# Top-p attention in layer 0: shorter lists, one evaluation counted instead of run, one sum taken by a product, and the adjacency marks spread from the front on

## The chip, the cores and the metric

The kernel runs on one core of one Trainium2 chip. The metric is the device time of one execution in microseconds (us); each kernel is run three times and the median is taken. Engines are named as the profile names them: PE (TensorE matmuls; PEld are its weight loads), DVE (VectorE), ACT (ScalarE), POOL (GpSimd) and SP (SyncE, which issues most DMAs here).

## What is computed

Four graph layers on 4096 nodes of 256 features. Each takes x, normalises it, applies relu, runs a layer and adds the result to x. Only the first layer is touched by the change, and it has two steps (n = 0, 1):

```python
for n in range(STEPS):                       # STEPS = 2
    A = _top_p_attention(Xa, W1, W2, W3)     # 4096 x 4096, TOP_P = 0.9
    Xf = R @ Xf                              # R: adj plus the diagonal, rows scaled to sum 1; sparse
    Xa = A @ Xa
    Z = Z + Xf @ U1[n].T + Xa @ U2[n].T
```

Top-p attention takes the softmax of q k^T in each row, keeps the largest entries until their sum, without the entry itself, has reached 0.9, and divides by the sum of what was kept. About one entry in a thousand of adj is not zero. Layers 2 to 4 are a graph convolution, graph attention with four heads, and a second convolution.

## The kernel before, in words

**Sorting is avoided.** For each block b of 128 rows (32 blocks) the kernel has e = exp(logit − guess), 128x4096, and looks for the threshold t below which entries are dropped. It does so in these parts, named as in the lists of the order further down:

- *logits* (PE, L1148) and *exps* (ACT, L1162): e, in two halves.
- *evaluations* (`evaluate`, ACT, L1178): s*k* counts the entries over a trial threshold by the sum of signs, r*k* gives the mass below it by a relu, each with an accumulated sum. k = 0, 1 read 1024 columns (1.15 us each in the profile), k = 2, 3 read all 4096 (3.71 us).
- *updates* (`first`, `second`, `third`; DVE, L1200 to L1252): each turns s*k*, r*k* into a better trial threshold, in a series of instructions on 128x1. `first` belongs to k = 0, `second` to 1, `third` to 2. After k = 3, `bound` (L1255) turns the last evaluation into *hi*, a threshold that should be a little above the final one: `AHEAD` sets the margin.
- *below* (DVE, L1331): the entries under hi, with their sum; *segments* (L1339): the 8 largest in each of 16 segments of 256; *listing* (`order`, L1343 to L1353): from these 128, in rounds of 8 (a MAX8, and a MATCH_REPLACE8 with the load of its values), the `LIST` largest in falling order; *decide* (L1358 to L1381): where in that list the sum reaches the goal, so the exact threshold.
- *cut* (DVE, L1401) sets the dropped entries of e to zero; *drop* (L1403) removes ties where there are any.
- *flip* (PE transposes, L1469), *take* (ACT, PSUM to SBUF, L1475), *attend* (PE, L1484), in eight groups of four: the product A Xa. *attended* (ACT, L1493) scales it.

Then, for the block's rows, *turn_pe* (PE, L1512) transposes the new rows (xa) and the old (h), *turn* (ACT, L1517) copies them out, *keys_pe* and *keys* compute the next step's keys and queries, *xa_pe* and *h_pe* (`weighted`, PE, L1523) multiply by U1 and U2, *copy_xa* (ACT, L1542), *store_xa* (DVE add, L1546) and *store_h* (ACT, L1536) bring the results to SBUF and start their stores.

**Order of work.** The queues are in program order: `ORDERS` (L1096) lists by hand, for a *period*, what is issued. A name stands for a call with block b plus the offset behind `@` (`s0@3` is block b + 3). One period per block and three lead-in periods, −3 to −1, so DVE, ACT and PE work on four blocks at a time. The first list is step 0's, the second step 1's; step 1 also gathers the sparse product R Xf on POOL and applies it on PE. `some` and `along` (L921) interleave several generators instruction by instruction: `order` is listing beside bound, `maxima` segments beside bound, `third` an update beside decide, `first` an update beside the scale of the next product.

**PSUM and buffers that matter here.** The transposed tiles (pat, pt, tag pmisc) have two buffers, `take` three SBUF buffers, `pu` and the keys' bank share one tag (pr), hu has two.

**Marks.** Beside step 0 the kernel finds where adj is not zero: for each block, four quarters of adj (128x1024, 512 KB each) are loaded by SP, and `mark` (L1495) reduces each half of a quarter, 128x512, to the largest absolute value of each column group: eight instructions on DVE (L1498) per block, 256 in all. At the end of step 0 `listed_columns` (L748) turns the marks into lists.

**Check at the end.** `verify` (L1443) notes for every row that its list was long enough and its margin held; where a row's wasn't, `general_layers` computes all layers again in a plain way.

Of the kernel before, what the change touches and what calls it, by code (L numbers as in the profile page):

```python
# [92 lines left out]
SEG = 16  # L93
LIST = 48
AHEAD = 16.0
HUGE = 3e38


QUARTERS = 4
CHUNKS = 5  # L100
CAP = 32 * CHUNKS

# [552 lines left out]
def fast_layers(  # L655
# [81 lines left out]

    def load_adj(pool, ib):

        parts = []  # L740
        for c in range(0, NB, CA):
            t = pool.tile([P, CA, P], F32, name="adj", tag="adj")
            nc.sync.dma_start(t, adjt[ib, :, c : c + CA, :])
            parts.append(t)
        return parts

# [280 lines left out]

    def front(h0, kt, xs):

# [26 lines left out]
        for i in range(NB + LAG + 4):  # L1056
            o = i - LAG
            if i < NB:
                six = sm.tile([P, 6], F32, name="six")
                nc.vector.bn_stats(six, x0[i // 16][:, i % 16, :])  # L1060
                nc.vector.bn_aggr(spread_[:, i, :], six)
                if i % 4 == 3:
                    group = slice(i - 3, i + 1)
                    var = sm.tile([P, 4], F32, name="var4")
                    nc.vector.tensor_scalar_add(var, spread_[:, group, 1], LN_EPS)
                    nc.gpsimd.tensor_tensor(scale[:, group, 0], var, minus_half[:, :4], op=ALU.pow)
            if 0 <= o + 1 < NB:
                relu(o + 1)
# [29 lines left out]
    opened below attend2@-1 s1@2 some_maxima flip4@-1 r1@2 flip5@-1 attend3@-1 take4@-1 take5@-1 flip6@-1  # L1098
    second attend4@-1 take6@-1 attend5@-1 mark s2@2 mark maxima fill flip7@-1 attend6@-1 take7@-1 r2@2 attend7@-1
    order early logits0@3 attended@-1 mark turn_pe@-1 third fill turn@-1 exps0@3 keys_pe@-1 ties_pe logits1@3 cut  # L1100
    keys@-1 ties exps1@3 xa_pe@-1 s0@3 mark r0@3 drop copy_xa@-1 s3@2 store_xa@-1 flip0 mark flip1 mark
    take0 h_pe@-1 take1 fill first r3@2 flip2 attend0 mark mark attend1 store_h@-1 take2 flip3 take3 fill
    """,
# [3 lines left out]
    exps1@3 stood@-3 cut mix0 s0@3 laid@-3 s3@2 projected@-3 finish@-1 level@-2 mixed0 drop mix1 tabled@-3  # L1107
    r0@3 r3@2 attend7@-1 shifted@-2 fill first flip0 spread0 flip1 take0 heads@-1 other1 s1@3 attend0 take1 r1@3 flip2 flip3
    take2 attend1 take3 flip4 attend2 flip5 fill
# [16 lines left out]
    def layer0_step(n, va, kt, own, extra=None):  # L1126
# [43 lines left out]
        def evaluate(b, k, funcs=(AF.Sign, AF.Relu)):  # L1170

            s = state[b]
            width = PART if k < 2 else N
            if AF.Sign in funcs:
                s["signs"], s["gap"] = small("signs"), small("gap")
                s.setdefault("at", ones)
            for func in funcs:
                nc.scalar.activation(  # L1178
                    unread[:, :width],
                    s["e"][:, :width],  # L1180
                    func,
                    bias=s["at"],
                    scale=-1.0,
                    accum_out=s["signs"] if func == AF.Sign else s["gap"],
                )
# [15 lines left out]
        def measured(b, k):  # L1201
# [16 lines left out]
            return low, steep, goal  # L1218

        def stepped(to, m, t):  # L1220

# [33 lines left out]
        def bound(b):  # L1255

            s = state[b]
            low, steep, goal = yield from measured(b, 3)
            t = s["at"]
# [19 lines left out]
            yield  # L1279
            nc.vector.tensor_scalar_add(square[:, 1:2], square[:, 1:2], 1e-4)  # L1280
            yield
            nc.vector.scalar_tensor_tensor(
                square[:, 0:1], power, 1e-4, square[:, 0:1], op0=ALU.mult, op1=ALU.add
            )
# [23 lines left out]
            ahead, inverse = small("ahead"), small("inverse")  # L1308
            nc.vector.scalar_tensor_tensor(ahead, final, AHEAD, by, op0=ALU.mult, op1=ALU.mult)
            yield  # L1310
            nc.vector.reciprocal(inverse, goal)
            yield
            nc.vector.tensor_scalar(ahead, ahead, inverse, 3.0, op0=ALU.mult, op1=ALU.min)
            yield
# [28 lines left out]
        def listing(b):  # L1343

            first = state[b]["best"].rearrange("p k m -> p (k m)")
            rest = wk.tile([P, SEG * 8], F32, name="rest")
            listed = tops[:, b % 4, 1:]
            for k in range(0, LIST, 8):
                src = rest if k else first
                nc.vector.max(listed[:, k : k + 8], src)  # L1350
                yield
                if k + 8 < LIST:
                    nc.vector.match_replace(rest, listed[:, k : k + 8], src, 0.0)  # L1353
                    yield

            nc.gpsimd.tensor_copy(least[:, b : b + 1], listed[:, LIST - 1 :])

        def decide(b):  # L1358

            s, col = state[b], slice(b, b + 1)  # L1360
            listed, hi, room = tops[:, b % 4, 1:], end["hi"][:, col], end["room"][:, col]
            nc.vector.tensor_sub(room, s["low"], s["full_goal"])
            yield
            ahead_of = wk.tile([P, LIST], F32, name="ahead_of")
            nc.vector.tensor_tensor_scan(
                ahead_of, tops[:, b % 4, :LIST], tops[:, b % 4, :LIST], 0.0, op0=ALU.add, op1=ALU.bypass
            )
            yield
            out_ = wk.tile([P, LIST], F32, name="out_")
            nc.vector.tensor_scalar(out_, ahead_of, room, None, op0=ALU.is_ge)  # L1370
            yield
            kept = wk.tile([P, LIST], F32, name="kept")
            nc.vector.scalar_tensor_tensor(kept, out_, HUGE, listed, op0=ALU.mult, op1=ALU.add)
# [120 lines left out]

        def mark(b):  # L1495
            for q in range(QUARTERS):
                for part in (slice(0, CA // 2), slice(CA // 2, CA)):
                    nc.vector.tensor_reduce(  # L1498
                        marks[:, part, q, b],
                        state[b]["adj"][q][:, part, :],  # L1500
                        AX.X,
                        ALU.max,
                        apply_absolute_value=True,
                    )
                    yield

        def turn(b):
# [11 lines left out]
        def weighted(b, v):  # L1519

            pu = ps1.tile([P, 2, D], F32, name="pu", tag="pr")
            for k in range(DC):
# [4 lines left out]
                    start=(k == 0),  # L1527
                    stop=(k == DC - 1),
                )
            state[b]["pu"] = pu  # L1530

# [8 lines left out]
        def copy_xa(b):  # L1540
            t = state[b]["hu"] = own.tile([P, 2, D + 1], F32, name="hu", bufs=2)
            nc.scalar.copy(t[:, 0, :D], state[b]["pu"][:, 0, :])  # L1542

        def store_xa(b):
            rows, t = slice(b * P, (b + 1) * P), state[b]["hu"]
            nc.vector.tensor_add(t[:, 1, :D], va[:, b, :], state[b]["pu"][:, 1, :])  # L1546
            nc.sync.dma_start(heads_d[rows, :], t[:, 0, :D])
# [182 lines left out]
        def opened(b):  # L1730
            if n == 0 and 0 <= b < NB:
                state[b]["adj"] = load_adj(extra, b)
            if n == 1 and b in (0, NB // 2 + 1):
# [41 lines left out]
        def of_pair(f, r):  # L1775
# [5 lines left out]
            "drop": of_block(drop),  # L1781
            "mark": lambda b: some(line(mark, b), 1),
            "attended": of_block(attended),
# [6 lines left out]
            "copy_xa": of_block(copy_xa),  # L1790
            "store_xa": of_block(store_xa),
            "store_h": of_block(store_h),
# [26 lines left out]

        def period(b, fill=(), pieces=(0, 0, 0, 0)):  # L1820


            pieces = iter(pieces)
            for name, off in tables[max(b - NB + 1, 0)]:
                if name == "fill":
                    some(fill, next(pieces))
                else:
                    calls[name](b + int(off))

        def close(lists):  # L1830
# [29 lines left out]
            copy_xa(last)  # L1860
            store_xa(last)
            guesses = guess(1, pm)
# [8 lines left out]
    with ExitStack() as st:  # L1871
# [5 lines left out]
        for i, u in enumerate((u1t, u2t)):  # L1877
            wu.append(s0.tile([P, DC, 2, D], F32, name=f"wu{i}"))
            for n in range(2):
                nc.sync.dma_start(wu[i][:, :, 1 - n, :], u[n].rearrange("(c p) m -> p c m", p=P))  # L1880
        with tc.tile_pool(name="front", bufs=1) as xs, tc.manual_schedule(engines=MANUAL):
            guesses = front(h0, kt0, xs)
        own = st.enter_context(tc.tile_pool(name="own0", bufs=1))
        adj_pool = st.enter_context(tc.tile_pool(name="adj0", bufs=4))
        with tc.manual_schedule(engines=MANUAL):
            period, verify, close = layer0_step(0, h0, kt0, own, adj_pool)
            for b in range(-3, NB):
                period(b, guesses, {-3: (0, 0, 3, 0), -2: (3, 9, 9, 9)}.get(b, (0, 0, 0, 0)))
            lists = listed_columns(marks, e_pool.tile([P, N], F32, name="e"), ps)
            guesses = close(lists)  # L1890

    with ExitStack() as st:
# [3 lines left out]
        with tc.manual_schedule(engines=MANUAL):  # L1896
# [3 lines left out]
            for b in range(-3, NB + 2):  # L1900
                period(b, fill, pieces.get(b, (0, 0, 0, 0)))
                if b == -1:
# [412 lines left out]
```

## Time and profile before

| | us |
|---|---|
| three runs, median (lowest to highest) | 3152.24 (3150.27 to 3155.07) |
| the profiled execution | 3154.33 |
| its span, first to last instruction | 3152.2 |
| PE busy | 2524.1 (80%) |
| DVE busy | 2555.9 (81%) |
| ACT busy | 2242.7 (71%) |
| POOL busy | 1274.5 (40%) |
| mean granted TensorE clock | 0.934 |

By the trace's cuts (L1401) the span has these stages: a front that normalises and makes keys (0 to 106), the lead-in of step 0 (106 to 193), step 0's periods (193 to 1188), its close and the lead-in of step 1 (1188 to 1326), step 1's periods (1326 to about 2400), and the other three layers (from 2400 on).

How to read it: the views used are the page, *windows* (busy time of each engine in a stretch, then the granted clock, the DMA's share and GB/s), *waits* (engine and line, what it waited for, us in total, times, longest), and the *timeline* of one engine (start, duration, instruction, count, and in brackets the idle time before it with what ended it). A shape is written partitions x elements. In the timeline, neighbouring instructions of one line are joined, and a duration runs over the next instruction's start where the engine overlaps them, so "spacing" (start to start) is said where it is meant.

### The profile page before, as it was taken

To read this page: it belongs to the slowest core of one execution; us is meant where nothing else is said; L and a number is where in the kernel's file an instruction comes from. 1 tells how busy PE (TensorE), PEld (TensorE's weight loads), DVE (VectorE), ACT (ScalarE), POOL (GpSimd) and SP (SyncE) were. 2 spreads that over 40 slices of the span, in tenths; PEclk is the share of its full clock that TensorE was granted. 3 is DMA by queue.
4 is the path that set the end of the run, shared out by engine and by line. 5 is a ranking of instruction groups with operands and counts; after the bars stand their busy time and mean duration, and the time that the engine had idled before them with its cause. 6 is when DMAs were issued, how large, how long until landed. Compare 5 with 4: busy or idle time off the path is not lost. (4 is left out here: it accounts for less than half of the span.)

```text
span 3152.2 us, 44347 instructions
## 1 busy us (share of the span) xinstructions
PE 2524.1 (80%) x12468; PEld 1893.4 (60%) x12468; DVE 2555.9 (81%) x9611; ACT 2242.7 (71%) x3436; POOL 1274.5 (40%) x1350
## 2 busy tenths in 40 slices
PE   6658888888888887398998988999876776888666
PEld 5336556565656665176767667677765554788444
DVE  3389999999999998899999999999982776899200
ACT  3589999999999953888888888998932123899100
POOL 1000000000000000278888846566654775775576
PEclk9779999999999999699999999999988998999888
DMA  3012232322223233034444433334333874554575
GB/s 125 9 48 88 78 98 77 96 81 84 88 76 98 78 111 98 29 111 126 126 125 126 124 106 107 104 97 127 109 94 95 266 212 136 150 157 123 177 210 163
DMA packets 213852, 357.05 MB, mean 113 GB/s; under 512 B 33879, under 2 KB 147036, under 8 KB 213596
## 3 DMA queue, kind: packets, MB, share of 16 engines
q1 hardware_dynamic: 169100, 237.74, 23.6%
q0 software_dynamic: 43520, 116.14, 13.6%
q8 instruction: 102, 1.67, 0.2%
q14 instruction: 154, 1.26, 0.1%
q10 hardware_dynamic: 976, 0.23, 0.0%
HBM read 290.85 MB, written 63.13 MB: 112 GB/s over the span
## 5 line engine op out<-in xcount | busy, mean ns | idle before, releaser
L1178 ACT ACTIVATE unread<-e,next_pair 128x4096 uint8<-128x4096 f32 (+1 forms) x384 | 1098.2, 2860 | 50.0 <-DVE next_pair L1229 45.3
L1484 PE MATMUL pa<-va,at 128*128 128x256 f32 x2048 | 498.7, 392 | 60.3 <-DVE t L1615 45.0
L1484 PE MATMUL pa<-h,at 128*128 128x256 f32 x2048 | 472.2, 381 | 17.5 <-ACT at L1475 17.5
L1484 PEld LDWEIGHTS pa<-va,at 128*128 128x128 f32 x2048 | 384.8, 195 | 142.4 <-ACT at L1475 61.0
L1341 POOL COPY eighth<-best 128x16 f32<-128x16 f32 x64 | 21.6, 337 | 1039.2 <-DVE best L1339 824.9
L1475 ACT COPY at<-pat 128x512 f32<-128x512 f32 x512 | 285.1, 583 | 197.8 <-PE pat L1469 192.7
L1484 PEld LDWEIGHTS pa<-h,at 128*128 128x128 f32 x2048 | 377.3, 190 | 69.3 <-ACT at L1475 24.4
L1339 DVE MAX8 best<-near 128x8 f32<-128x256 f32 x1024 | 404.5, 418 | 3.2
L1469 PE MATMUL pat<-ident,e 128*128 128x128 f32 x2048 | 291.7, 279 | 100.4 <-ACT at L1475 55.1
L1469 PEld LDWEIGHTS pat<-ident,e 128*128 128x128 f32 x2048 | 247.3, 144 | 185.9 <-ACT at L1475 79.3
L835 POOL DMA_INDIRECT vg<-v_d,column x320 | 306.1, 956 | 118.7 <-issue 90.6
L1148 PE MATMUL pl<-kt,qb 64*128 64x512 f32 x1024 | 279.2, 656 | 75.8 <-ACT e L1162 75.7
L1162 ACT ACTIVATE e<-pl,minus_guess 128x1024 f32<-128x1024 f32 x256 | 282.9, 1111 | 44.7 <-PE pl L1148 34.3
L850 PE MATMUL acc<-vg,ac 128*128 128x256 f32 x768 | 228.9, 445 | 93.1 <-DMA vg<-v_d,column 73.0
L1331 DVE SCALAR_TENSOR_TENSOR near<-e,end_hi 128x4096 f32<-128x4096 f32 x64 | 286.7, 4480 | 0.1
L1401 DVE SCALAR_TENSOR_TENSOR e<-e,end_t 128x4096 f32<-128x4096 f32 x64 | 286.6, 4478 | 0.0
L835 POOL DMA_INDIRECT vg<-far_d,column x160 | 250.4, 1565 | 60.2 <-issue 41.8
L835 POOL DMA_INDIRECT vg<-mixed_d,column x160 | 219.1, 1369 | 86.2 <-issue 44.6
L850 PEld LDWEIGHTS acc<-vg,ac 128*128 128x128 f32 x768 | 157.9, 220 | 158.6 <-DMA vg<-v_d,column 100.6
L850 PE MATMUL pr<-vg,ac 128*128 128x257 f32 (+1 forms) x768 | 197.5, 409 | 56.1 <-issue 33.8
L2141 PE MATMUL acc<-u,tabg 128*65 128x128 f32 x1536 | 194.5, 281 | 45.3 <-DVE u L2126 44.2
L850 PEld LDWEIGHTS pr<-vg,ac 128*128 128x128 f32 x768 | 150.4, 202 | 104.8 <-issue 39.5
(554 smaller groups left out, 4483.7 us busy)
## 6 DMA issues: line engine op xcount, KB each, us to landing
adj<-in_adjt SPq DMA_DIRECT2D x128, 512.0 KB
ac<-adjc_d SPq DMA_DIRECT2D x96, 384.0 KB
adjc_d<-ac SPq DMA_DIRECT2D x32, 384.0 KB
vg<-v_d SPq DMA_DIRECT2D x64, 128.0 KB
targets<-steep_d SPq DMA_DIRECT2D x32, 256.0 KB
vg<-v_d,column POOLq DMA_INDIRECT x320, 4.0
table_d<-tab SPq DMA_DIRECT2D x32, 132.0 KB
tabg<-table_d SPq DMA_DIRECT2D x32, 132.0 KB
```

Of the source, the lines that this page charges most:

```text
L835: nc.gpsimd.indirect_dma_start(out, None, rows, bass.IndirectOffsetOnAxis(ap=index, axis=0))
L850: nc.tensor.matmul(acc, ac[:, k, :], v[:, k, :], start=(k == 0), stop=(k == CHUNKS and not own))
L1148: nc.tensor.matmul(pl[:, r, :], s["qb"][rows], kt[rows, j * 512 : (j + 1) * 512], start=True, stop=True,)
L1162: nc.scalar.activation(s["e"][:, j * 1024 : (j + 1) * 1024], pl.rearrange("p r c -> p (r c)"), AF.Exp, bias=minus_guess[:, b : b + 1], acc ...
L1178: nc.scalar.activation(unread[:, :width], s["e"][:, :width], func, bias=s["at"], scale=-1.0, accum_out=s["signs"] if func == AF.Sign else ...
L1331: nc.vector.scalar_tensor_tensor(near, s["e"], end["hi"][:, b : b + 1], s["e"], op0=ALU.is_lt, op1=ALU.mult, accum_out=s["low"])
L1339: nc.vector.max(best[:, k, :], near[:, k * (N // SEG) : (k + 1) * (N // SEG)])
L1401: nc.vector.scalar_tensor_tensor(s["e"], s["e"], last, s["e"], op0=ALU.is_ge, op1=ALU.mult, accum_out=s["held"])
L1469: nc.tensor.transpose(pt[:, k, :], s["e"][:, c * P : (c + 1) * P], ident)
L1475: nc.scalar.copy(at, s["pt", g])
L1484: nc.tensor.matmul(s["pa"], s["at", g][:, k, :], va[:, c, :D], start=(c == 0), stop=(c == NB - 1))
L2141: nc.tensor.matmul(s["acc"][:, h, :], s["tab"][:, k, h * (DK + 1) : (h + 1) * (DK + 1)], s["u"][:, k, h, :], start=(k == 0), stop=(k == CH ...
```

## The change

It changes layer 0 in these places.

- **Marks.** A generator, `marking`, walks over all 128 quarters in order; it keeps the loads up to four quarters ahead and makes one reduce of a whole quarter (128x8 from 128x1024) per step. `mark` in the list takes one step of it. 16 steps are taken in the front, 4 more in the front's end, 36 by the `fill` places of the lead-in periods, and three in each period from block 0 on (before: eight half reduces in each), until the 128 are used up.
- **r3 is not run.** The relu evaluation for k = 3 leaves the lists, in both steps. `counted` takes its place: it works the mass out from the last two counts (s2 and s3), the two thresholds and the mass before.
- **Lists of 32 and 40.** `LIST` = 48 becomes 32 in step 0 and 40 in step 1: four and five rounds of listing instead of six. The margin of `bound` has another formula, with `AHEAD` 11 in place of 16 and a term from the last step's size.
- **store_xa's add becomes a product.** In `weighted(b, 0)` one more matmul adds the identity times the block's old rows into the second half of pu, and `copy_xa` copies both halves (128x512 in place of 128x256). The add on DVE goes.
- **copy_xa is issued earlier**, directly after exps1 and xa_pe and ahead of s0, r0 and drop; before, it stood behind them. The two stores come with it.

The diff, cut to its core:

```diff
-LIST = 48
-AHEAD = 16.0
+LISTS = (32, 40)
+LIST = max(LISTS)
+AHEAD = 11.0
+SPREAD = 0.5
...
-    def load_adj(pool, ib):
+    def marking(pool, marks):
         parts = []
-        for c in range(0, NB, CA):
-            t = pool.tile([P, CA, P], F32, name="adj", tag="adj")
-            nc.sync.dma_start(t, adjt[ib, :, c : c + CA, :])
-            parts.append(t)
-        return parts
+        for k in range(NB * QUARTERS):
+            while len(parts) < min(k + ADJ_BUFS, NB * QUARTERS):
+                b, q = divmod(len(parts), QUARTERS)
+                parts.append(pool.tile([P, CA, P], F32, name="adj"))
+                nc.sync.dma_start(parts[-1], adjt[b, :, q * CA : (q + 1) * CA, :])
+            b, q = divmod(k, QUARTERS)
+            nc.vector.tensor_reduce(
+                marks[:, :, q, b], parts[k], AX.X, ALU.max, apply_absolute_value=True
+            )
+            yield
...
+            if i >= 10 and i % 2 == 0:
+                some(marked, 1)
...
-    second attend4@-1 take6@-1 attend5@-1 mark s2@2 mark maxima fill flip7@-1 attend6@-1 take7@-1 r2@2 attend7@-1
-    order early logits0@3 attended@-1 mark turn_pe@-1 third fill turn@-1 exps0@3 keys_pe@-1 ties_pe logits1@3 cut
-    keys@-1 ties exps1@3 xa_pe@-1 s0@3 mark r0@3 drop copy_xa@-1 s3@2 store_xa@-1 flip0 mark flip1 mark
-    take0 h_pe@-1 take1 fill first r3@2 flip2 attend0 mark mark attend1 store_h@-1 take2 flip3 take3 fill
+    second attend4@-1 take6@-1 attend5@-1 mark s2@2 maxima fill flip7@-1 attend6@-1 take7@-1 r2@2 attend7@-1
+    order early logits0@3 attended@-1 turn_pe@-1 third fill turn@-1 exps0@3 keys_pe@-1 ties_pe logits1@3 cut
+    keys@-1 ties exps1@3 xa_pe@-1 copy_xa@-1 s0@3 r0@3 mark drop s3@2 flip0 flip1
+    take0 h_pe@-1 take1 fill first flip2 attend0 mark attend1 store_h@-1 take2 flip3 take3 fill
...
-    r0@3 r3@2 attend7@-1 shifted@-2 fill first flip0 spread0 flip1 take0 heads@-1 other1 s1@3 attend0 take1 r1@3 flip2 flip3
+    r0@3 attend7@-1 shifted@-2 fill first flip0 spread0 flip1 take0 heads@-1 other1 s1@3 attend0 take1 r1@3 flip2 flip3
...
+        def counted(b):
+            s = state[b]
+            pair, before, goal = s["next"], s["before"], s["full_goal"]
+            s["pair"] = pair
+            t, low, twice, steep = pair[:, 0:1], pair[:, 1:2], small("twice"), small("steep")
+            mass, gap = small("mass"), small("gap")
+            nc.vector.tensor_add(mass, t, before[:, 0:1])
+            yield
+            nc.vector.scalar_tensor_tensor(
+                mass, s["signs"], s["signs2"], mass, op0=ALU.subtract, op1=ALU.mult
+            )
+            yield
+            nc.vector.tensor_scalar(twice, s["signs"], float(N), t, op0=ALU.add, op1=ALU.mult)
+            yield
+            nc.vector.scalar_tensor_tensor(
+                low, mass, 0.25, before[:, 1:2], op0=ALU.mult, op1=ALU.add
+            )
+            yield
+            nc.vector.scalar_tensor_tensor(low, goal, 0.1, low, op0=ALU.mult, op1=ALU.max)
+            yield
+            nc.vector.scalar_tensor_tensor(gap, twice, 0.5, low, op0=ALU.mult, op1=ALU.subtract)
+            yield
+            nc.vector.scalar_tensor_tensor(
+                steep, gap, -0.33 / 0.465, twice, op0=ALU.mult, op1=ALU.add
+            )
+            yield
+            s["gap"] = gap
+            return low, steep, goal
...
         def bound(b):
-            low, steep, goal = yield from measured(b, 3)
+            low, steep, goal = yield from counted(b)
...
-            nc.vector.scalar_tensor_tensor(ahead, final, AHEAD, by, op0=ALU.mult, op1=ALU.mult)
+            nc.vector.scalar_tensor_tensor(m, m, -1.0, m, op0=ALU.mult, op1=ALU.max)
+            yield
+            nc.vector.scalar_tensor_tensor(
+                ahead, final, AHEAD / (4.0 * SPREAD), by, op0=ALU.mult, op1=ALU.mult
+            )
...
-            nc.vector.tensor_scalar(ahead, ahead, inverse, 3.0, op0=ALU.mult, op1=ALU.min)
+            nc.vector.scalar_tensor_tensor(ahead, ahead, inverse, m, op0=ALU.mult, op1=ALU.add)
+            yield
+            nc.vector.tensor_scalar(ahead, ahead, 4.0 * SPREAD, 3.0, op0=ALU.mult, op1=ALU.min)
...
-            for k in range(0, LIST, 8):
+            for k in range(0, LISTS[n], 8):
...
-                if k + 8 < LIST:
+                if k + 8 < LISTS[n]:
...
         def weighted(b, v):
...
-                    stop=(k == DC - 1),
+                    stop=(k == DC - 1 and v > 0),
                 )
+            if v == 0:
+                nc.tensor.matmul(pu[:, 1, :], ident, va[:, b, :], start=False, stop=True)
...
         def copy_xa(b):
             t = state[b]["hu"] = own.tile([P, 2, D + 1], F32, name="hu", bufs=2)
-            nc.scalar.copy(t[:, 0, :D], state[b]["pu"][:, 0, :])
-
-        def store_xa(b):
-            rows, t = slice(b * P, (b + 1) * P), state[b]["hu"]
-            nc.vector.tensor_add(t[:, 1, :D], va[:, b, :], state[b]["pu"][:, 1, :])
+            nc.scalar.copy(t[:, :, :D], state[b]["pu"])
+            rows = slice(b * P, (b + 1) * P)
             nc.sync.dma_start(heads_d[rows, :], t[:, 0, :D])
             nc.sync.dma_start(base_d[rows, :], t[:, 1, :D])
...
+            early = {
+                -3: ((0, 2), (0, 2), (3, 2), (0, 2)),
+                -2: ((3, 4), (9, 4), (9, 4), (9, 4)),
+                -1: ((0, 3), (0, 3), (0, 3), (0, 3)),
+            }
             for b in range(-3, NB):
-                period(b, guesses, {-3: (0, 0, 3, 0), -2: (3, 9, 9, 9)}.get(b, (0, 0, 0, 0)))
+                period(b, (guesses, marked), early.get(b, ((0, 0),) * 4))
```

## The prediction

> **What bounds the kernel now.** The profiled execution took 3154.3 us (span 3152.2), 2.1 above the median of the runs shown, 3152.24; the sum is made on 3154.3. The page's chain follows only the last 16 us of the span, so I read by stage: the windows view for which engine is full, the waits of each stage, then the timeline of one period, engine by engine. The windows (PE, PEld, DVE, ACT, POOL busy, then the granted clock) of step 0 and step 1:
>
> ```profile
> 600.00:800.00 200.00, 171.76 (x836) 121.36 (x835) 188.89 (x768) 184.56 (x242) 2.73 (x18) 1.00 0.26 84
> 1330.00:1700.00 370.00, 326.21 (x1569) 253.44 (x1570) 358.25 (x1350) 326.13 (x370) 296.53 (x249) 0.96 0.42 121
> ```
>
> In step 0 DVE is 94% busy, but it isn't the bound: the waits of 300 to 1100 us show it stopped once in each period by ACT, and ACT hardly ever by DVE.
>
> ```profile
> DVE hu L1546 <- ACT hu L1542: 26.2, 24, 1.2
> ACT unread L1178 <- DVE m L1301: 0.3, 1, 0.3
> ```
>
> A period is the distance of two cuts (L1401): 32.41 us on average over the 28 from 226.97 to 1134.40. ACT's timeline in one of them (start, us, ...):
>
> ```profile
> 646.31 0.59 ACT L1517 COPY zt<-pt 128x512 f32<-128x512 f32 x1 [0.74 <-PE pt L1512]
> ...
> 651.80 1.13 ACT L1178 ACTIVATE unread<-e,ones 128x1024 uint8<-128x1024 f32 x1
> ...
> 654.20 0.35 ACT L1542 COPY hu<-pu 128x256 f32<-128x256 f32 x1
> 654.46 3.71 ACT L1178 ACTIVATE unread<-e,next_pair 128x4096 uint8<-128x4096 f32 x1
> ...
> 658.16 1.06 ACT L1475 COPY at<-pat 128x512 f32<-128x512 f32 x2
> 659.10 3.72 ACT L1178 ACTIVATE unread<-e,next_pair 128x4096 uint8<-128x4096 f32 x1
> ...
> 663.27 1.10 ACT L1475 COPY at<-pat 128x512 f32<-128x512 f32 x2
> ```
>
> In the order of the list these are turn, s0 and r0, copy_xa, s3, take0 and take1, r3, take2 and take3. PE beside it:
>
> ```profile
> 650.21 1.98 PE L1523 MATMUL pu<-wu,zt 128*128 128x512 f32 x4
> 653.46 1.09 PE L1469 MATMUL pat<-ident,e 128*128 128x128 f32 x8 [1.27 <-DVEq L1408]
> 655.06 1.98 PE L1523 MATMUL pu<-wu,zt 128*128 128x512 f32 x4 [0.51 <-DVE hu L1546]
> 658.78 0.66 PE L1469 MATMUL pat<-ident,e 128*128 128x128 f32 x4 [1.74 <-ACT at L1475]
> ...
> 663.93 1.99 PE L1484 MATMUL pa<-h,at 128*128 128x256 f32 x8 [0.60 <-ACT at L1475]
> ...
> 678.16 0.44 PE L1512 MATMUL pt<-ident,xa 128*128 128x128 f32 x2
> ```
>
> They are xa_pe, flip0 and flip1, h_pe, flip2, attend2, turn_pe. From flip2 to turn_pe PE works without a gap except for attend2, which waits for take2 behind r3. flip2 needs one of two PSUM buffers, so it waits for take0; take0 stands behind s3. The loop closes: turn_pe to zt's start 0.69, to s0 5.49 (both exps, keys), s0 and r0 2.40, copy_xa 0.26, s3 3.70, take0 to flip2 0.62: 13.16 (645.62 to 658.78). PE from flip2 to the next turn_pe: 19.4, of which 0.76 is the wait for take2 (weights' wait included) and 18.65 PE's own. 13.16 + 18.65 + 0.76 = 32.57, the measured period within 0.2. So **step 0 is bound by a loop through ACT and PE**; DVE has 1.2 us of slack.
>
> Step 1 is different: windows of its periods show DVE 97% busy, its waits with DVE ahead hold 0.3 to 0.8 us, and POOL's gathers run beneath. There DVE is the bound.
>
> **Part by part.**
>
> *r3 goes* (L1178, 3.71 + 0.19, 64 times), and counted adds six small DVE instructions. In step 0 the loop contains only 0.76 of r3, the wait of attend2: −0.76. The six (0.12 spacing each, rows of 0.15 us) are taken in turn with the rounds of listing, whose gaps hold most of them; I take 0.1 to 0.4 a period, with no end in step 0, where DVE has the slack.
>
> *copy_xa moves ahead of s0 and r0, and becomes 128x512.* Before, it stood behind r0, when xa_pe (650.21 to 652.19) had long ended, and waited for nothing. Now ACT reaches it at the end of exps1 (651.80, turn_pe + 6.18) and must wait for xa_pe: + 6.57, + 0.44 for the added product (two records as L1512's, 0.22 apart), + 0.13 to a copy's start as in the rows: turn_pe + 7.05. Wait: **+0.87**. Queued behind it on ACT: s0, r0, s3, take0, and so flip2. The wide copy costs 0.48 in place of 0.26 (L1517's copy of that size, by its spacing): +0.22. Bounds: +0.9 to +1.2 for both. The stores of heads_d and base_d move ahead with it. On SP they can stand behind a load of a quarter that waits for the reduce just before it; hu has two buffers, so a store has most of a period before a copy misses it: 0.
>
> *Loop without a change of clock:* 32.57 − 0.76 + 0.87 + 0.22 = 32.9, or +0.33 a period, +10 us over 28 periods: nothing of r3's 3.9 us is won, as what follows is s3 before take0.
>
> *The clock.* After the change PE runs flip0, flip1 and h_pe earlier: flip0 and flip1 no longer wait for the cut, as DVE is ahead, and h_pe waits for copy_xa, not for L1546. It ends at turn_pe + 10.3 (copy_xa's end 7.5, flips' 1.0, 1.83), flip2 starts at turn_pe + 13.16 + 1.09 = 14.25: PE stands still for **3.95 us** in each period, where it stood for 1.74 before. What that does shows in step 1. Windows and PE there:
>
> ```profile
> 1617.00:1620.40 3.40, 3.40 (x16) 2.15 (x15) 3.30 (x15) 2.93 (x5) 2.79 (x3) 1.00 0.96 309
> 1620.40:1623.80 3.40, 1.12 (x6) 0.63 (x4) 3.37 (x6) 3.37 (x3) 3.40 (x1) 1.00 0.20 63
> 1623.80:1627.20 3.40, 3.29 (x8) 2.67 (x9) 3.40 (x3) 3.33 (x5) 2.63 (x6) 0.52 0.49 135
> ...
> 1623.91 4.53 PE L850 MATMUL pr<-vg,ac 128*128 128x257 f32 x12 [2.40 <-issue]
> ```
>
> A window with PE busy for a third (one gap of 2.40) is followed by one of the granted clock at half, and the same twelve products took 4.53 in it, 2.88 just before: 1.65 lost. Over the trace the granted clock changes on a grid of 3.41 us; full-speed windows busy for 42% or less are nearly all followed by a half-speed one, those from 49% on in step 0 never (its clock is 1.00 all through). A gap of 3.95 leaves some window 58% idle or more wherever the grid falls, so the drop should come in nearly every period, right where flip2 starts the PE part of the loop. A half-speed window holds 1.7 us less work; laid out against the grid the period becomes 34.7, **+2.2 × 28 = +62** in place of +10. Bounds: +10 (no drop) to +80 (a second window in one period of three).
>
> The Trainium skill ("TensorE: Matmul & The Clock Gate", "HAM oscillation — how this bites in real kernels") rules that only PE idle gaps above some 3.4 us bring the throttle back, a wholly idle window by its Part 1. By that rule a gap of 3.95 covers a whole window in (3.95 − 3.41) / 3.41 = 16% of phases, an estimate of +9 on top of the +10; this trace throttled after 2.3 to 2.4, so the trace decides.
>
> *Marks.* 256 reduces of 0.60 spacing become 128 of 128x1024: nearest row L797 (same elements read, 1.22 us), about 1.15 by spacing. The work is equal; it moves. Sixteen go into the front, where DVE is 30 to 45% busy: 0, and its tail 0.8. Of the early ones 28 fall in periods −2 and −1 (135 to 193), DVE busy 34.4 of 58 there: 34.4 + 28 × 1.15 − 2 (marks already there) = 64.6, 6.6 over; and DVE can't fill the gaps at its six updates, where it waits about 1 to 1.3 us each for s and r (rows of 0.94 and 1.06): +7. **+14**, bounds +5 (r3's 3.9 gone from ACT lets the chain catch up) to +20 (512 KB loads supplied late, 1.8 us each). Afterwards three a period, under the slack: 0.
>
> *Lists of 32 and 40:* two rounds less in step 0, one in step 1 (MAX8, load, replace: 0.72 spacing). Step 0: 0, DVE isn't the bound. Step 1: −0.72 − 0.04 + 0.2 for counted = −0.55 × 30 = **−16.5** (bounds −8 to −24: PE's half clocks there may take some back). r3's going gives ACT 3.9 us that step 1 doesn't wait for: 0.
>
> *Product for the add L1546* (423 ns): its stall of 1.23 on DVE goes; late next is the third update's wait for r2. Loop: counted above. *Close:* −0.4; *step 1's start:* −2 (r3 before s1, a longer chain in bound). *Layers 1 to 3:* 0.
>
> **Sum:** 3154.3 + 0.8 + 14 + 62 − 16.5 − 0.4 − 2 = **3212 us**.
>
> **Rivals.**
>
> *The clock holds.* Step 0's lowest windows now (49% busy) passed, and if the gap comes out at 2 us, not 3.95, so do these. Then 3154.3 + 0.8 + 14 + 10 − 16.5 − 2.4 = 3160, with the bounds of marks and step 1 3144 to 3172. It decides when PE's gap before flip2 stays under about 2.
>
> *Faster: DVE is step 0's bound after all.* 94% busy speaks for it. If take0 is not what flip2 waits for, the period falls with DVE's: 32.41 − 1.44 (two rounds) − 1.6 (the add and its stall) − 1.3 (marks, 8 × 0.60 to 3 × 1.15) + 0.4 = 28.5, or −110: 3150 (the sum without step 0's loop) − 110 = 3040; with half of it kept, as PE and ACT have 27 and 26 us of work each, 3095. Against it: flip2 and attend2 wait for ACT in these periods, and DVE's stall is itself a wait for ACT. It decides when flip2 starts less than about 12 us behind turn_pe.
>
> *A step is repeated.* Were a list too short for one row, the general path would compute the layers again, by estimate at least the 3154 us of the listed way. Worked out from the inputs, no row needs more than 28 of 32 and 38 of 40 entries; 1%.
>
> **How the numbers follow.** Forecast (half clock in most periods) 65%, own range 3190 to 3232; clock holds 17%; faster 13%; other slower ones 4%, repeat 1%. The range 3140 to 3236 leaves out the faster case, the repeat and a few per cent of tails. What a measurement here can tell from no change is 0.2%, 6.3 us: 3146 to 3158.5 around the median. The clock case lies half in it: same 8%; faster 13% + 2%; slower the rest.
>
> **What would show it.** In step 0: cuts about 34.7 apart; PE idle 3.9 before flip2, for ACT at L1475; granted clock near 0.95 in windows now at 1.00; ACT waiting 0.8 at copy_xa for PE; DVE idle some us a period, for ACT. Step 1's periods 0.5 shorter. The first cut (now 193.44) near 207 to 210. It is wrong if the clock of step 0 stays 1.00, or if its period falls under 32.

## The result, and the profile after

The changed kernel takes 3204.99 us (median of four runs, 3202.86 to 3207.61) against 3151.55 for the kernel before on the same chip: ratio 1.0168, 95% interval 1.0151 to 1.0186. It is slower by 53 us; the forecast was 3212. The profiled execution has a span of 3200.8 us, 48.6 more than before's. Between the same cuts of both traces:

| stage | before, us | after, us | difference | forecast |
|---|---|---|---|---|
| front and lead-in, up to the first cut | 193.4 | 211.2 | +17.8 | +14.8 |
| step 0, first cut to 30th | 941.0 | 1005.2 | +64.2 | +62 |
| end of step 0, close, lead-in of step 1 | 192.0 | 188.8 | −3.2 | −2.4 |
| step 1, first cut to last | 1035.0 | 1013.4 | −21.6 | −16.5 |
| the rest (layers 2 to 4) | 790.8 | 782.2 | −8.6 | 0 |

(In the changed kernel the cut is L1449, evaluations L1190, flip L1517, attend L1532, take L1523, turn L1553, xa_pe and h_pe L1559 with the added product L1567, copy_xa L1580, marks L750, below L1379.)

The windows of steps 0 and 1 after (PE, PEld, DVE, ACT and POOL busy, granted clock, DMA share, GB/s):

```profile
600.00:800.00 200.00, 168.57 (x783) 123.00 (x784) 164.81 (x689) 154.79 (x209) 2.73 (x18) 0.94 0.21 65
1390.00:1760.00 370.00, 318.45 (x1529) 244.25 (x1530) 360.88 (x1457) 289.00 (x349) 299.62 (x253) 0.95 0.43 121
```

In step 0 no engine is full any more: DVE went from 94% to 82%, ACT from 92% to 77%, and the period still grew from 32.41 to 34.74. Work left, and the loop got longer. The clock is 0.94 where it was 1.00. In step 1 DVE is as full as before (97.5%). The waits of step 0, from 300 to 1150 us (engine, what it waited for, us in total, times, longest):

```profile
PE pat L1517 <- ACT at L1523: 108.7, 24, 4.7
DVE twice L1220 <- ACT unread L1190: 83.7, 49, 4.1
DVE pair L1222 <- ACT unread L1190: 48.6, 49, 1.0
ACT hu L1580 <- PE pu L1567: 21.5, 24, 1.0
```

PE waits 4.5 us for take0 once in each period, where it waited 1.7; DVE now waits for ACT's evaluations; copy_xa waits 0.9 for xa_pe. ACT's and PE's timelines over one period show the gap and what comes behind it:

```profile
666.01 0.59 ACT L1580 COPY hu<-pu 128x512 f32<-128x512 f32 x1 [0.76 <-PE pu L1567]
...
669.04 3.71 ACT L1190 ACTIVATE unread<-e,next_pair 128x4096 uint8<-128x4096 f32 x1
...
672.75 1.05 ACT L1523 COPY at<-pat 128x512 f32<-128x512 f32 x2
```

```profile
666.98 1.88 PE L1559 MATMUL pu<-wu,zt 128*128 128x512 f32 x4
673.37 1.12 PE L1517 MATMUL pat<-ident,e 128*128 128x128 f32 x4 [4.51 <-ACT at L1523]
674.28 4.53 PE L1532 MATMUL pa<-h,at 128*128 128x256 f32 x16
...
707.61 1.12 PE L1517 MATMUL pat<-ident,e 128*128 128x128 f32 x4 [4.51 <-ACT at L1523]
708.51 6.17 PE L1532 MATMUL pa<-h,at 128*128 128x256 f32 x16
```

h_pe ends at 668.86, flip2 starts at 673.37. The sixteen products behind it take 4.53 us in this period and 6.17 in the next; at full clock they took 3.62. Half speed runs from 672.7 to 676.1 here. Two stretches across the gap, which lie 1.1 us behind the grid on which the clock changes, so that each holds a part of it:

```profile
670.40:673.80 3.40, 0.43 (x2) 0.43 (x3) 3.37 (x4) 3.40 (x5) 0.00 (x0) 0.84 0.29 67
673.80:677.20 3.40, 3.40 (x14) 2.91 (x13) 3.30 (x6) 1.08 (x3) 0.00 (x0) 0.66 0.49 175
```

The granted clock is at half for one stretch of 3.4 us in most periods: these cuts are 34.24 to 34.6 apart. In about every sixth period it stays at half for 6.8, and the cuts are 35.9 apart (35.0 in the last such case). In these six the gap reaches further into the first half-speed stretch: PE is busy for 77 to 78% of it in five of them and for 26% in the sixth, while after stretches busy for 80% or more the clock came back. Half-speed time in the 28 periods is 116 us; before it was 2.

### The profile page after: what moved, and what is told of

It is laid out like the page before. It is cut to its first block, busy times and chain, and to the rows that moved or that the text cites. A ratio compares the mean times of both kernels' runs of the same rounds, so it can differ in the third digit from the quotient of the medians.

```text
span 3200.8 us, 44193 instructions
## 1 busy us (share of the span) xinstructions
PE 2553.5 (80%) x12532; PEld 1929.9 (60%) x12532; DVE 2511.2 (78%) x9547; ACT 2022.3 (63%) x3308; POOL 1266.8 (40%) x1350
## 5 line engine op out<-in xcount | busy, mean ns | idle before, releaser
L1190 ACT ACTIVATE unread<-e,next_pair 128x4096 uint8<-128x4096 f32 (+1 forms) x320 | 859.7, 2686 | 103.5 <-DVE next_pair L1271 71.2
L1532 PE MATMUL pa<-va,at 128*128 128x256 f32 x2048 | 495.5, 389 | 55.7 <-DVE t L1650 47.8
L1523 ACT COPY at<-pat 128x512 f32<-128x512 f32 x512 | 287.8, 581 | 391.8 <-PE pat L1517 386.3
L1532 PE MATMUL pa<-h,at 128*128 128x256 f32 x2048 | 511.9, 405 | 0.0
L1532 PEld LDWEIGHTS pa<-va,at 128*128 128x128 f32 x2048 | 381.4, 193 | 138.1 <-issue 46.7
L1532 PEld LDWEIGHTS pa<-h,at 128*128 128x128 f32 x2048 | 409.8, 207 | 57.5
L1517 PE MATMUL pat<-ident,e 128*128 128x128 f32 x2048 | 299.9, 284 | 143.6 <-ACT at L1523 132.2
L1517 PEld LDWEIGHTS pat<-ident,e 128*128 128x128 f32 x2048 | 252.9, 147 | 212.9 <-ACT at L1523 156.6
L1379 DVE SCALAR_TENSOR_TENSOR near<-e,end_hi 128x4096 f32<-128x4096 f32 x64 | 286.7, 4480 | 0.1
L1449 DVE SCALAR_TENSOR_TENSOR e<-e,end_t 128x4096 f32<-128x4096 f32 x64 | 286.6, 4478 | 0.0
L2180 PEld LDWEIGHTS acc<-u,tabg 128*65 128x65 f32 x1536 | 172.3, 141 | 64.7 <-DVE u L2165 53.5
```

Source lines behind the costliest of these rows:

```text
L1190: nc.scalar.activation(unread[:, :width], s["e"][:, :width], func, bias=s["at"], scale=-1.0, accum_out=s["signs"] if func == AF.Sign else ...
L1379: nc.vector.scalar_tensor_tensor(near, s["e"], end["hi"][:, b : b + 1], s["e"], op0=ALU.is_lt, op1=ALU.mult, accum_out=s["low"])
L1449: nc.vector.scalar_tensor_tensor(s["e"], s["e"], last, s["e"], op0=ALU.is_ge, op1=ALU.mult, accum_out=s["held"])
L1517: nc.tensor.transpose(pt[:, k, :], s["e"][:, c * P : (c + 1) * P], ident)
L1523: nc.scalar.copy(at, s["pt", g])
L1532: nc.tensor.matmul(s["pa"], s["at", g][:, k, :], va[:, c, :D], start=(c == 0), stop=(c == NB - 1))
```

## The experiments

All of them ran on a second chip, in two batches. The kernel before takes 3427.56 us there in the first (warm PE, copy_xa back, takes first, marks late) and 3406.50 in the second (the other four). The chips differ by stage: the changed kernel's step 0 is as on the first chip, but step 1's first half takes some 40 us a period, not 32, and the rest took 890 to 907 in the eight runs, not 782 to 791. So the experiments are read by stage, and times only against the kernel before of the same batch. The times of warm PE, marks late and lists of 48 are single executions; those of the kernel before spread from 3416.59 to 3435.05 in the first batch. For the kernel before, the stages are known from the first chip alone.

**The changed kernel again.** No edit.

> The changed kernel once more, to have its stages and time on this chip beside the kernel before and the others. Theory: step 0's period 34.74 and first cut at 211 whatever the chip; step 1 and the later layers as this chip's gathers make them.

Measured: first cut at 211.2, step 0's period 34.67; the time 3468.56, 62 over before (ratio 1.0186, interval 1.0164 to 1.0208). For the changed kernel, step 0 and the lead-in are the same on both chips.

**A warm PE.** Is the clock the cause, or only there as well? h_pe's products are issued three times into the same place:

```diff
             state[b]["pu"] = pu
+            if v and b < NB - 1:
+                for _ in range(2):
+                    for k in range(DC):
+                        nc.tensor.matmul(
+                            pu.rearrange("p u d -> p (u d)"),
+                            state[b]["zt"][:, 2 * v + k, :],
+                            wu[1 - v][:, k].rearrange("p u d -> p (u d)"),
+                            start=(k == 0),
+                            stop=(k == DC - 1),
+                        )
```

> The changed kernel with h_pe's four products (h rows by U2, 1.83 us) issued three times over into the same PSUM tile, the last overwriting the first two: 3.7 us more work for PE, placed in the 4.5 us in which it stands still ahead of flip2; nothing else changes. Theory (the idle gap makes the clock drop, and the drop costs the 1.8 us by which the period exceeds the loop's sum of 32.9): granted clock 1.00 in step 0, period 32.8 to 33.0 in place of 34.74, time about 3205 - 28 x 1.8 = 3154. Rival (the period is longer because copy_xa's wait and something behind it on ACT are longer than worked out, and the clock is a symptom): period 34.7 or more, as PE has only more to do, time 3205 or more.

The window of step 0:

```profile
600.00:800.00 200.00, 189.06 (x877) 130.12 (x876) 173.23 (x713) 164.04 (x226) 2.96 (x19) 1.00 0.22 69
```

One wait between 300 and 1150 us, PE for take0 (1.1 a period, where it was 4.5):

```profile
PE pat L1517 <- ACT at L1523: 28.9, 26, 1.3
```

Period 32.92, clock 1.00, no half-speed time in 28 periods: 3.6 us more work on PE made the period 1.75 us shorter than the same chip's 34.67. So the loop without the clock is 32.9, as worked out, and the clock's drop is the rest. The rival, that something on ACT was longer than thought, falls. The time, 3442.97 (one run), is 15 over before in its batch, where the changed kernel is 62 over in its own: 47 less, and 28 × 1.75 is 49.

**copy_xa back behind r0.**

```diff
-    keys@-1 ties exps1@3 xa_pe@-1 copy_xa@-1 s0@3 r0@3 mark drop s3@2 flip0 flip1
+    keys@-1 ties exps1@3 xa_pe@-1 s0@3 r0@3 mark drop copy_xa@-1 s3@2 flip0 flip1
```

> The changed kernel with copy_xa and its two stores put back behind r0 and drop, as before. Theory: ACT no longer waits 0.87 for xa_pe; loop 32.9 - 0.87 = 32.0; h_pe waits for copy_xa, ends 1.1 later, and flip2 comes 0.87 earlier, so PE's gap ahead of flip2 falls from 4.5 to about 2.0; a window is then 41% busy at the least, at the edge of where the clock drops: it stays full in six periods of ten or more. Period 32.0 to 32.8, time 3130 to 3150. Rival (the place of copy_xa is not what made the gap; r3's going alone did): gap over 3.5 and period 34 or more, time 3185 to 3205.

Windows and one line of PE's timeline:

```profile
600.00:800.00 200.00, 176.68 (x827) 124.50 (x827) 172.39 (x711) 162.06 (x225) 2.99 (x20) 0.97 0.21 68
```

```profile
647.27 0.66 PE L1517 MATMUL pat<-ident,e 128*128 128x128 f32 x4 [2.19 <-ACT at L1523]
```

The gap is 2.19, in between; and so is the clock: the distances of the cuts fall into two groups, 31.6 to 31.9 in 11 of the 28 periods and 33.3 to 33.6 in 17. Half-speed time is 58 us, 17 stretches of 3.4. A drop costs 1.7 us, a gap of 2.2 brings one in six of ten periods; more than expected (four of ten). The mean is 32.77, at the long end of what was expected. The time, 3429.58, is level with the kernel before's (1.0015, 1.0003 to 1.0027), where the changed kernel is 62 over: putting copy_xa back takes 1.9 us off each period of step 0, most of the 2.3 that the change lost there.

**take0 and take1 ahead of s3.**

```diff
-    keys@-1 ties exps1@3 xa_pe@-1 copy_xa@-1 s0@3 r0@3 mark drop s3@2 flip0 flip1
-    take0 h_pe@-1 take1 fill first flip2 attend0 mark attend1 store_h@-1 take2 flip3 take3 fill
+    keys@-1 ties exps1@3 xa_pe@-1 copy_xa@-1 s0@3 r0@3 mark drop flip0 flip1
+    take0 h_pe@-1 take1 s3@2 fill first flip2 attend0 mark attend1 store_h@-1 take2 flip3 take3 fill
```

> The changed kernel with take0 and take1 issued ahead of s3 on ACT, not behind it. Theory (the loop goes through s3 to take0 to flip2): take0 starts at turn_pe + 9.9 in place of 13.6, flip2 follows h_pe without a gap, the clock stays 1.00; attend2 then waits for take2 behind s3 by 0.8. Loop 10.5 + 18.65 + 0.8 = 30.0; period 29.8 to 30.8, time 3205 - 28 x 4.3 = 3085 (3065 to 3100). Rival (another chain bounds step 0, DVE or second - s2 - r2 - third, near the old 32.4): period 32 or more, time 3130 or more, with PE waiting elsewhere.

Period 31.28, clock 1.00, the time 3393.32 (0.990 of before, 0.9883 to 0.9916). The main point holds: with take0 freed PE waits for it 0.5 us a period, where it was 4.5 (300 to 1150 us):

```profile
PE pat L1517 <- ACT at L1523: 12.2, 26, 0.9
```

The period is half a us over the expected range, so another chain came up. ACT, and DVE in the period's first part:

```profile
670.23 3.71 ACT L1190 ACTIVATE unread<-e,next_pair 128x4096 uint8<-128x4096 f32 x1 [1.66 <-DVE by L1333]
```

```profile
658.90 1.22 DVE L750 TENSOR_REDUCE marks<-adj 128x8 f32<-128x1024 f32 x1
660.03 4.48 DVE L1379 SCALAR_TENSOR_TENSOR near<-e,end_hi 128x4096 f32<-128x4096 f32 x1
```

s2 now waits 1.66 for DVE's second update. DVE comes to it from the first update, which waits for r0, by way of a mark, below and the first maxima: a loop through both engines, with the mark in it. In the periods in which no marks are left the distance is 30.29, that is 1.13 less, one mark.

**Marks late.** No marks in the front and the lead-in; four in each period:

```diff
-            if i >= 10 and i % 2 == 0:
-                some(marked, 1)
...
-                -2: ((3, 4), (9, 4), (9, 4), (9, 4)),
-                -1: ((0, 3), (0, 3), (0, 3), (0, 3)),
+                -2: ((3, 0), (9, 0), (9, 0), (9, 0)),
+                -1: ((0, 0), (0, 0), (0, 0), (0, 0)),
```

(and 0 in period −3, one more `mark` behind s2 in the list).

> The changed kernel with no marks in the front and the lead-in periods, and four in each period of step 0 in place of three. Theory (the early marks lengthen the lead-in, and marks are free under step 0's slack): the first cut at 193 to 197 in place of 211, step 0's period unchanged at 34.7, the last two periods as before (27 in place of 22.4, +9), the close about as it is; time 3205 - 16 + 9 = 3198 (3190 to 3203). Rival (the lead-in is longer for another reason, r3's going or the changed clock): first cut stays at 205 or later, time 3205 or more.

First cut at 186.2, which is 25 earlier than with the marks, not 16: the lead-in without them is 7 shorter than before's, which r3's going brought (the kernel before without r3, further down, has its first cut at 185.5), and the early marks cost all of 25. Step 0's period is 34.72, so a fourth mark is free there; the last two periods are 51.8 in place of 44.7 together. The time, 3466.68 (one run), is 39 over before, 23 less than the changed kernel's 62; 25 − 7 is 18. The rival falls. ACT's waits for DVE in the last 27 us before the first cut, in the changed kernel (first fence) and in this one:

```profile
184.69 3.71 ACT L1190 ACTIVATE unread<-e,next_pair 128x4096 uint8<-128x4096 f32 x1 [4.27 <-DVE next_pair L1271]
196.02 1.15 ACT L1190 ACTIVATE unread<-e,next_pair 128x1024 uint8<-128x1024 f32 x1 [7.54 <-DVE next_pair L1271]
201.57 3.71 ACT L1190 ACTIVATE unread<-e,next_pair 128x4096 uint8<-128x4096 f32 x1 [3.03 <-DVE total L1313]
```

```profile
176.02 3.71 ACT L1188 ACTIVATE unread<-e,next_pair 128x4096 uint8<-128x4096 f32 x1 [2.06 <-DVE total L1311]
```

With early marks ACT stands 4.3, 7.5 and 3.0 us for DVE, without them 2.06 once.

**Lists of 48.**

```diff
-LISTS = (32, 40)
+LISTS = (48, 48)
```

> The changed kernel with lists of 48 in both steps. Theory (step 1 is DVE's, step 0 is not): step 0's period stays 34.74 although DVE gets two rounds (1.44) more; step 1's periods 0.72 longer than the changed kernel's on a chip where they are bound by DVE (31.8 and 33.8 become 32.5 and 34.5), about 22 in all; where the gathers bind step 1's first half, only the second half. Rival (step 1's gain came from r3's going, by 3.9 us less on ACT): step 1 moves by less than 0.2 a period.

Step 0's period 34.72: two rounds more on DVE cost nothing there. In step 1's second half (the ten periods before the last two) a period takes 35.28 against 34.56 of the changed kernel in this batch: +0.72, one round. By itself that isn't safe: the four variants of the first batch, with lists of 40 and the same code in step 1, take 35.07 to 35.16 there. The last period of step 1 settles it. With lists of 40 it takes 33.68 to 33.73 in all seven runs, on both chips; with lists of 48 it takes 34.44 in the kernel before, 34.46 here and 34.49 in the next run, in which r3 is gone as well (with counted in its place). So a round is 0.75 there and r3's going brings nothing: the rival falls for the end of step 1. Step 1's first half is the same in both (40.5), as something else binds it on this chip; for it only the first chip's −0.6 a period speaks. The time, 3487.98 (one run), is 19 over the changed kernel's.

**The kernel before, with only r3 taken out.**

```diff
-            low, steep, goal = yield from measured(b, 3)
+            low, steep, goal = yield from counted(b)
...
-    take0 h_pe@-1 take1 fill first r3@2 flip2 attend0 mark mark attend1 store_h@-1 take2 flip3 take3 fill
+    take0 h_pe@-1 take1 fill first flip2 attend0 mark mark attend1 store_h@-1 take2 flip3 take3 fill
```

(the same in step 1's list, and the changed margin).

> The kernel before with r3 left out in both steps and counted in its place (with the changed margin), all else as before: lists of 48, half-quarter marks, add on DVE, copy_xa behind r0. Theory (step 0's loop holds only 0.76 of r3): period 31.6 to 31.9 in place of 32.41, clock 1.00 in step 0, first cut 4 to 7 earlier than 193.4; step 1 0 to +0.2 a period (six small instructions on DVE); about 18 to 25 less than before. Rival (r3 is 3.9 us of the bound): step 0's period 29 to 30, 70 less or more. Second rival (r3's going alone opens the gap that drops the clock): period 33 or more.

Windows of step 0, and two of its waits (ACT for the second update, DVE for copy_xa):

```profile
600.00:800.00 200.00, 175.65 (x835) 120.06 (x833) 191.85 (x810) 165.11 (x229) 3.01 (x20) 0.98 0.27 84
```

```profile
ACT unread L1181 <- DVE by L1324: 21.7, 25, 1.1
DVE hu L1585 <- ACT hu L1581: 19.4, 25, 0.9
```

Period 32.23, only 0.17 less than 32.41, where 0.5 to 0.8 was expected; first cut 185.5, 8 earlier; the time 0.9975 of before (0.9959 to 0.9991), 8 us less where 18 to 25 was expected. Both rivals fall: 3.9 us of ACT's work leave each period, and neither 3.9 come off nor does PE's gap before flip2 pass 1.7. But the theory had too much slack for DVE: it is 96% busy now, and s2 waits 0.9 for it in each period, where before there was one wait of 0.3. Just under the loop of ACT and PE lies the loop of DVE and ACT that the takes-first run showed.

The clock didn't stay at 1.00 as expected: it fell to half in four of the 28 periods, each time after a window in which PE was busy for 48% and had no gap over 1.6 us. One of them, at 387.2 to 390.6:

```profile
385.70 1.09 PE L1508 MATMUL pat<-ident,e 128*128 128x128 f32 x8 [1.60 <-DVEq L1447]
386.98 3.60 PE L1562 MATMUL pu<-wu,zt 128*128 128x512 f32 x4 [0.18 <-DVE hu L1585]
```

Here h_pe takes 3.60 in place of 1.98, but it runs in the time in which flip2 waits for take0 otherwise, and the four periods (32.35 to 32.43) are no longer than their neighbours. So a drop seems to cost only what such a wait doesn't take up; that is read from these four periods, not tried.

**Takes first, and the marks moved.** This puts together what the runs point to:

```diff
-    second attend4@-1 take6@-1 attend5@-1 mark s2@2 maxima fill flip7@-1 attend6@-1 take7@-1 r2@2 attend7@-1
+    second attend4@-1 take6@-1 attend5@-1 s2@2 mark mark maxima fill flip7@-1 attend6@-1 take7@-1 r2@2 attend7@-1
...
-    keys@-1 ties exps1@3 xa_pe@-1 copy_xa@-1 s0@3 r0@3 mark drop s3@2 flip0 flip1
-    take0 h_pe@-1 take1 fill first flip2 attend0 mark attend1 store_h@-1 take2 flip3 take3 fill
+    keys@-1 ties exps1@3 xa_pe@-1 copy_xa@-1 s0@3 r0@3 mark drop flip0 flip1
+    take0 h_pe@-1 take1 s3@2 fill first flip2 attend0 attend1 store_h@-1 take2 flip3 take3 fill
...
-                -2: ((3, 4), (9, 4), (9, 4), (9, 4)),
-                -1: ((0, 3), (0, 3), (0, 3), (0, 3)),
+                -2: ((3, 1), (9, 1), (9, 1), (9, 1)),
+                -1: ((0, 0), (0, 0), (0, 0), (0, 0)),
```

> The changed kernel with take0 and take1 ahead of s3, the mark that stood between the first update and below moved behind the second (two marks there), and four marks in the lead-in (periods -2 and -1) in place of 28; the front's marks and those of period -3 stay. Theory (with takes first, the loop is first - below - second - s2 - r2 - exps - s0 - r0, and the mark behind first is 1.13 of its 31.42, as it fell to 30.29 where the marks ran out): period 30.3, clock 1.00 in step 0, first cut near 190, last two periods +7 (marks now last longer); against the changed kernel on the same chip -28 x 4.4 - 20 + 7 = -136. Rival (something else holds 31.4, as PE's loop): period 31.2 or more. Where step 1 is as in the changed kernel's profile, about 3070.

```profile
600.00:800.00 200.00, 183.60 (x893) 129.10 (x892) 186.80 (x761) 177.11 (x244) 3.21 (x21) 1.00 0.24 74
```

Period 30.32, first cut at 187.0, 1 us of half clock in 28 periods; the time 3314.40 against 3406.50: ratio 0.9722 (0.9701 to 0.9743), and 154 less than the changed kernel in the same batch, where 136 was expected. With the same parts in another order the change is faster than the kernel before by 92 us on this chip. What the order alone would bring, in the kernel before with r3 and its other parts, was not run.

## Why the prediction was right, point by point

- **What bounds step 0: right.** The loop turn_pe, exps, s0, r0, s3, take0, flip2, and PE's products back to turn_pe. Freeing take0 from s3 freed the loop; taking r3 away moved the period by 0.17, not by 3.9. The loop's own −0.76 doesn't show in that run, as another loop took over; it fits the eleven periods without a drop in the copy_xa-back run (32.41 − 0.76 + 0.22 = 31.87; 31.6 to 31.9 measured). The "1.2 us of slack" given to DVE was too much: with r3 alone gone DVE's own loop holds at 32.2.
- **copy_xa's wait, +0.87 and +0.22: right.** 0.76 to 0.9 measured, and the loop with the clock held came out at 32.92, worked out as 32.9. Two slips stand behind that match. The terms given for copy_xa's start add up to turn_pe + 7.14, not 7.05; the trace has 7.04. And the loop was added up from 32.57, not from the measured 32.41: the change was worked out as +0.33 and is +0.51. No run takes the added product or the wide copy out alone.
- **The gap and the clock, +2.2 a period: right, and the largest term.** The gap is 4.51, not 3.95: h_pe ended at turn_pe + 9.9 (10.3 worked out) and flip2 began at + 14.4 (14.25). The 28 periods hold 34 half-speed stretches of 3.4 us, one in each and a second in every sixth or so; the period is 34.74, worked out as 34.7. The warm PE shows that it is the clock, and that it is 1.75 to 1.8 of the 2.33.
- **The rule of the skill** (the Trainium skill, "TensorE: Matmul & The Clock Gate", "HAM oscillation — how this bites in real kernels"): the page says "no PE-idle gaps >~3.4µs"; that shorter gaps do no harm was the prediction's reading of it. The runs go against that reading: with copy_xa back, all 17 drops follow windows in which PE was busy for 36 to 40%, with no gap over 2.19. The estimate of +9 fails for a second reason: it took the gap to fall on all phases of the grid alike. Ten windows are 34.13 us and most periods 34.24 to 34.6, so the gap keeps nearly the same place for several periods, and 19 of the changed kernel's 28 drops follow a window in which PE stood still for all but 0.01 us, which the rule covers. The other nine follow windows busy for 13 to 35%. The clock's part came to 49 us (28 × 1.75), not 9.
- **Early marks, +14: right in sign, too small.** They cost 25, and r3's going gives back 7. "r3's 3.9 gone from ACT lets the chain catch up" was used as a bound only; and the price of a mark ahead of an update was put too low, as ACT and DVE follow one another in the lead-in: a mark ahead of an update holds the update up, and ACT behind it. The last kernel shows which marks cost it: it keeps the twenty of the front, the eight of period −3 and four of the 28 in periods −2 and −1, and its first cut, 187.0, is only 0.8 later than without any (with takes first and all the early marks it is 210.6). So the 24 marks left out cost about 24 us, nearly a full mark (1.13 by spacing) each: next to nothing of them fitted into DVE's idle time, and the others were free.
- **Step 1, −16.5: −21.6.** 0.67 a period in place of 0.55; the round of the list is 0.72 to 0.75, worked out as 0.72 (second half and last period). The 0.2 that counted was to cost there is 0.1 at most; half-clock time fell from 89 to 70 us as well.
- **The rest, 0: −8.6, and open.** The change does not touch it. Kernels with the same code there spread over 16 us on the second chip (890.6 to 906.7), so one profile each can't tell. Row by row, the front, the lead-in and step 0 came out 5 us dearer than forecast and the stages behind them 14 us cheaper; that the time lies within 7 us of the forecast is in part luck.
- **The rivals.** "The clock holds" is the warm PE's case, and its 32.9 came out. "Faster, as DVE is the bound": did not happen, but its condition, flip2 not waiting for take0, is what the last kernel makes true, with 30.3, near the "half of it kept" that was priced.

## What to carry to other kernels

An engine at 94% need not be the bound: follow a period's loop from instruction to instruction, and count an instruction's going only by what it holds in that loop. When work leaves, look where the time goes that it filled: here it became an idle gap of TensorE, and the lower clock behind it cost more than the wait itself. Before an instruction is taken out, it's worth moving those that others queue behind (the copy ahead of s0 and r0, s3 ahead of take0): in the changed kernel, putting s3 behind two takes turned 62 us lost into 34 won.

## What the runs showed of the hardware that was not expected

- The granted clock drops for gaps well under one window of 3.41 us: in all 28 periods with a gap of 4.51, in 17 of 28 at 2.19, in none at 1.08 (warm PE). Near the edge one gap doesn't tell: in the kernel before a gap of 1.74 in windows 49% busy brought none (2 us of half clock at the end of the 28 periods), while without r3 four windows 48% busy, with no gap over 1.60, did.
- One drop cost 1.7 us in a period of 32 with copy_xa back, and nothing visible in the run without r3, where it fell into time in which PE waits for ACT anyway.
- More work on an engine can shorten the time: 3.6 us of products computed for nothing, in each period, took 1.75 off it.
- On the second chip the same code of step 1 took some 40 us a period in its first half in place of 32. In its profile DVE stands still there between neighbouring small instructions with no other engine of the core named as what it waits for (0.4 to 1.7 us in one period), and POOL waits 10 us for PE in most periods. What makes it so was not tried.
